# Group-norm statistics of three jobs on ScalarE, and weight batches, stores and sums at other steps of an attention pipeline

## The chip, the core and the metric

The kernel runs on one core of a Trainium2 chip. The metric is the device time of one execution in microseconds; lower is better. Engines are named as the profile names them: PE is TensorE (PEld its weight loads), DVE is VectorE, ACT is ScalarE, POOL is GpSimd, SP is SyncE, which issues most DMAs.

## The reference

Eight images of 512 channels and 32 x 32 positions, all float32, go through two layers. Each layer is a group norm over 8 groups, an attention with 8 heads of 64 channels over the 1024 positions, an output projection and a residual sum:

```
xg   = x.reshape(B, 8, -1)
xn   = (xg - xg.mean(-1)) * rsqrt(xg.var(-1) + 1e-5)      # then gamma, beta
q, k, v = Wq xn + bq, Wk xn + bk, Wv xn + bv              # 512 x 512 each
attn = softmax(q^T k / 8)                                  # per head, 1024 x 1024
x    = x + Wp (attn v) + bp
```

Layer 1 does the same with weights of its own. The output is x after both layers.

## The kernel before, in words

**Jobs.** A job is one image in one layer; there are 16, numbered n = 0 to 15, in the order image 0 layer 0, image 1 layer 0, image 0 layer 1, image 1 layer 1, then images 2 and 3 and so on. The program is a loop over n: the attention of job n, then the products that belong to the output projection O of job n and to V, K and Q of job n + 1. The order of instructions on PE, DVE and ACT is written out by hand; SP and POOL follow the program's order too.

**Projections.** The 512 x 512 weight products use Strassen's seven products at two levels, so each weight block is held as seven combined blocks per level. The combinations of the weights are made once for each layer by `factor` (L162 to L168, four DVE operations), stored to DRAM, and fetched again by later jobs (`w<-deep`, L189). From job 2 on V too has two levels (`DEEP_V = 2`); for job 1 it has one. On the side of the activations, `combine` (L423 to L429) makes the first level's sums of xn in the tile `t`, and `inner_sums` (L482 to L488) the second level's in the tile `deep`. Tiles of the name `round`, `raw` and `deep` share one buffer, in turns.

**Weight batches.** `put_round` (L1563) loads in jobs 0 to 3 one raw weight matrix for the round listed in `ROUNDS`, makes its factors by eight DVE operations, `first` and `second` (four of 128 x 512, four of 128 x 896), and stores seven tiles with DMAs on ACT's queue (`deep<-round`, L235). `put_first` (L1576) in jobs 0 and 1 loads one raw matrix (`raw<-wqkv_dram`), makes four factors (128 x 512) and stores them (`keep<-raw`).

**Attention.** `run` (L1258) goes through 64 steps: eight groups g (a pair of heads and half of the queries) of eight key blocks kc. Step i computes the scores of block i into a PSUM tile of two banks (two such tiles exist), ACT takes the exponential into a tile `e` (L1104), and PE multiplies the exponentials of step i - 2 with V (`po`, L1152). The 12 buffers of `e` are also those of the fetched weights and of partial products. The softmax sums are taken over the `e` tiles of a group: DVE adds them into `acc` (L1118, L1120), but the first `pairs(g)` pairs are first summed by POOL with an accumulating DMA (`e<-e`, L1129), and DVE adds each such sum at its due step, seven after (L1132). The last due add is followed by the reduction (L1190, `r`). Two groups share what follows: `gather` (three DMAs on SP, `r<-r`, L1213), about 7.6 us later by the program's own count `invert` (DVE, `lt` and on, L1217 to L1237, then DMAs `rd<-rt` and `rb<-rd`, L1230 and L1232), and `normalise` (DVE, L1247) at 16.2. `take` copies half of `po` on ACT (`px`, L1176) and adds on DVE (L1178).

**Beside attention.** Other work is put at given steps through tables: `put` fills `chores` (one function to a step; a taken step pushes the next one on), `move` fills `moves` (mostly DMAs). At step i `run` first does the attention's own work, then `chores[i]`, then `moves[i]`. Among it is the group norm of job n + 1 (class `Norm`):

- reads: `stat` (L279, bn_stats over 128 x 512 on DVE, then an aggregate L283), eight calls at steps 3 to 10, and `gather` (SP: `dm<-mv` L320, `gm<-dm` L324);
- `groups` (five small DVE operations, L331 to L335, a power on POOL, L336, and DMAs `dg<-ga` L338 and twice `mr<-dg` L341);
- `factors` (three small DVE operations, L349 to L351) and four times `apply` on ACT (L356, 128 x 1024);
- then the four `combine` sums.

The class also has a second way to read the statistics, which job 0 uses for a quarter of its channels: `sums` (L289, ACT, Identity with accumulation), `less_mean`, `squares` (L297, ACT, Square with accumulation and the negated mean as bias), `by_count`. Both write their element outputs into the tile `xn`, where `apply` overwrites them.

**After attention.** The last attention groups' sums, the output sums `os` (L593 to L598) and the partial products' additions follow on DVE, with a planner that keeps a clock of its own. Its entries are the same before and after.

Of the kernel before, what the change touches and what calls it, by code (L numbers as in the profile page):

```python
# [27 lines left out]
NC = C // P  # L28
# [25 lines left out]
DEEP_V = 2  # L54
ROUNDS = {0: (O, 0), 1: (V, 1), 2: (O, 1), 3: (V, 0)}
FIRST = {0: (K, 1), 1: (Q, 1)}
OUTER_V = (1, 6, 7, 2, 3, 5, 4)


# [22 lines left out]
def fast_path(  # L82
# [317 lines left out]
    def norm_steps(n):  # L400
        norm = Norm(n)

        def place():
            xn[0] = acts.tile([P, NC, S], F32, tag="xn", name=f"xn_{n}")

        def factors():
            norm.factors(slice(0, NC))
            place()

        reads = [lambda cc=cc, sh=sh: norm.stat(cc, sh) for cc in range(NC) for sh in range(2)]  # L410
        reads.append(norm.gather)
        steps = [norm.groups, factors] + [lambda cc=cc: norm.apply(cc) for cc in range(NC)]
        return reads, steps
# [664 lines left out]
    class Attention:  # L1078
# [43 lines left out]
        def pairs(self, g):  # L1122
            if g + 1 == len(self.groups):
                return 0
            return 3 if self.n < 2 and 0 < g < 5 else 2

        def add_pair(self, i):
            g, kc = self.steps[i]
# [126 lines left out]
            for at, step in zip(times, (gather, invert, spread, normalise)):  # L1255
                later(at, step)

        def run(self, chores, moves, taken=False):  # L1258


            steps = self.steps
            self.add(1)
            self.add(2)
            self.values(0)
            for at in (chores, moves):
                if 2 in at:
                    at[2]()
            for i in range(3, len(steps) + LEAD):
                if i < len(steps):
                    self.scores(i)  # L1270
                self.values(i - LEAD)
                g, kc = steps[i - LEAD]
                if kc % 2 == 1 and kc < 2 * self.pairs(g):
                    self.add_pair(i - LEAD)
                if i in self.due:
                    self.due.pop(i)()
                if kc == NT - 1:
                    if taken and g + 1 == len(self.groups):
                        self.reduce(g)
                    else:  # L1280
                        self.finish(g)
                    advance(0.85)
                for at in (chores, moves):
                    if i in at:
                        at[i]()
                advance(1.71)
# [141 lines left out]
    norm = Norm(0)  # L1428
# [116 lines left out]
    for n in range(-1, len(jobs)):  # L1545
        last = n + 1 == len(jobs)
        outs = None
        if n >= 0:
            chores, moves = {}, {}

            def put(i, fn):
                while i in chores:
# [9 lines left out]

            def put_round(which, layer):  # L1563
                load, first, second, stores = deep_round(which, layer)
                begin = {0: 6, 1: 12}.get(n, 9)
                move(begin, load)
                at = begin + 3
                for fn in first:
                    at = put(at + 1, fn)
                for fn in second:  # L1570
                    at = put(at + 1, fn)
                at = max(at + 3, 25)
                for i, fn in enumerate(stores):
                    at = move(at + 1 + i % 2, fn)

            def put_first(which, layer):  # L1576
                at = move(37 if n == 0 else 3, lambda: start()) + 3
                box = []

                def start():  # L1580
                    box.append(acts.tile([P, NW, 2, CH], F32, tag="deep", name=f"raw_{n}"))
                    load_blocks(box[0], layer, which)

                for part in range(4):
                    at = put(at + 1, lambda part=part: factor(box[0], part))
                move(at + 1, lambda: store_factors(box[0], layer, which))

            if last:
                w = last_weights(n)
                for part in range(4):  # L1590
                    put(12 + 2 * part, lambda part=part: factor(w, part))
                for i, fn in enumerate(last_sums(0)):
                    put(49 + 3 * i, fn)
            else:
                for i, (_, fn) in enumerate(extra):
                    put(2 + i, fn)
                if n == 1:
                    at = (8, 14, 15, 16, 18, 19, 21, 24, 27, 30)
                else:
                    for i, fn in zip((3, 3, 4, 5, 5, 6, 7, 7, 8), reads):  # L1600
                        put(i, fn)
                    at = (16, 22, 23, 24, 26, 27, 29, 31, 33, 35)
                    if n < DEEP_V + 2:
                        at = (17, 23, 24, 25, 27, 28, 30, 32, 34, 36)
                for i, fn in zip(at, steps):
                    put(i, fn)
                if n == 1:
                    put_first(*FIRST[n])
                if n in ROUNDS:
                    put_round(*ROUNDS[n])  # L1610
                if n == 0:
                    put_first(*FIRST[n])
                for i, fn in zip(at[len(steps) :], sums(n + 1)):
                    put(i, fn)
                put(48, lambda q=att.q: out_combine(q, None, 0))
                deep_first = deep_steps(n + 1)
                if n + 1 >= DEEP_V:
                    for i, fn in enumerate(deep_first):
                        put((42 if n in ROUNDS else 37) + 2 * i, fn)
                else:  # L1620
                    for at, fn in zip((50, 52, 54, 56), deep_first[4:]):
                        put(at, fn)
                move(58, lambda: extend_plan(n + 1))
                for _ in range(RING):
                    move(58, fetch)
            assert max([*chores, *moves], default=0) < NT * len(att.groups) + LEAD
            if n + 1 >= DEEP_V and not last:
                outs = OutputSums(n)
                ahead = deque()
                if jobs[n][1] == 1 and jobs[n][0] + 2 < B:  # L1630
                    ahead.extend(load_steps(jobs[n][0] + 2))
                both, plan_sums = deep_phases(n + 1, ahead, outs)

                att.run(chores, moves, True)
                extra = ahead
                plan_sums()
                banks(0, "one")
                if n + 2 < len(jobs):
                    reads, steps = norm_steps(n + 2)
                att.take(len(att.groups) - 1, both[0])  # L1640
                banks(1, "one")
                for thunk in both[1:]:
                    thunk()
                banks(0, "two")
                att = Attention(n + 1)
                att.scores(0)
                att.scores(1)
                banks(1, "two")
                att.scores(2, "po")
                continue  # L1650
            att.run(chores, moves)
            banks(0, "one")
            banks(1, "one")
            if last:
# [285 lines left out]
```

## Time and profile before

| what | value |
|---|---|
| median of 3 runs | 3186.69 us (3186.46 to 3188.62) |
| profiled execution, its own time | 3189.37 us |
| its span, first to last instruction | 3187.6 us |
| PE busy | 3155.9 us, 99% |
| DVE, ACT, POOL busy | 82%, 73%, 9% |
| mean granted PE clock | 0.997 |
| `w<-deep` fetches, `e<-e` sums, `deep<-round` stores | 399, 232, 28 DMAs |

Start and end of one execution of a job are easiest seen in the scores (L1099): step 3 of job 0 starts at 83.3 us, of job 1 at 293.0, of job 2 at 498.7, of job 3 at 699.1, of job 4 at 899.4, and from there every 195.6 us. A line of busy time by stretch gives the stretch, its length, then the busy time and the instructions in brackets for each engine, the granted PE clock, the DMA engines' busy share and GB/s. A line of waits gives the engine, the line that waited, what it waited for, the total in us, how often and the longest. A line of the timeline gives the start, the length, the engine, the line, the operation and, in square brackets, how long the engine had been idle and what released it.

### The profile page before, as it was taken

The numbers are of one execution on the slowest core, as the hardware profiler recorded it, in microseconds if no ns is written. First come the engines' busy times: TensorE is split into PE (matmuls) and PEld (weight loads), VectorE is DVE, ScalarE is ACT, GpSimd is POOL, SyncE is SP. The second block draws the span as 40 slices with busy tenths as digits, with TensorE's granted clock in tenths as the row PEclk, the third lists the DMA queues.
The fourth block names the chain that finished last, engine by engine and source line by source line (L and its number), as shares of the span: only waits on it lengthen the run. The fifth ranks groups of instructions, "written<-read, shape, count | busy, mean of one in ns | idle before, by whom it ended". The sixth has DMA issues, their size and how long they took to land.

```text
span 3187.6 us, 62162 instructions
## 1 busy us (share of the span) xinstructions
PE 3155.9 (99%) x24093; PEld 1873.2 (59%) x24093; DVE 2628.9 (82%) x3563; ACT 2334.8 (73%) x4234; POOL 290.8 (9%) x326
## 2 busy tenths in 40 slices
PE   9999999999999999999999999999999999999999
PEld 7366384573845738466393664837548375573844
DVE  8796798978979788797887969789697887978867
ACT  6657677686876868778687776867768677686874
POOL 0200101011000010100101010010000100001000
PEclk9999999999999999999999999999999999999999
DMA  7755765565645455355564545445556463444733
GB/s 276 165 141 156 161 204 137 150 195 134 203 106 142 122 101 183 73 147 164 130 199 81 157 101 143 125 94 170 136 140 179 88 193 75 132 127 95 221 75 82
DMA packets 187342, 454.51 MB, mean 143 GB/s; under 512 B 38056, under 2 KB 54304, under 8 KB 187040
## 3 DMA queue, kind: packets, MB, share of 16 engines
q0 software_dynamic: 50000, 153.64, 26.5%
q1 hardware_dynamic: 133008, 283.98, 26.2%
q10 hardware_dynamic: 4032, 12.85, 1.1%
q8 instruction: 192, 3.15, 0.4%
q14 instruction: 110, 0.90, 0.1%
HBM read 247.41 MB, written 48.17 MB: 93 GB/s over the span
## 4 chain that ended last, share of the span: by engine, by line
PE 76%; DVE 1%; issue 0%; ACT 0%; DVEq 0%
PE sc L1099 22%; PE po L1152 21%; PE zd L806 8%; PE vd L806 8%; PE yd L806 4%; PE ud L806 3%; PE vd L801 3%; PE zd L801 3%; PE yd L801 1%; PE ud L801 1%; DVE acc L1120 0%; PE z_last L1042 0%; DVE acc L1132 0%; DVE x L1064 0%; PE y_last L1042 0%
## 5 line engine op out<-in xcount | busy, mean ns | idle before, releaser
L1104 ACT ACTIVATE e<-sc 128x1024 f32<-128x1024 f32 x1024 | 1043.7, 1025 | 578.6 <-PE sc L1099 545.9
L1099 PE MATMUL sc<-q,k 64*64 64x512 f32 x8192 | 1059.8, 590 | 9.1 <-ACT e L1104 9.1
L1152 PE MATMUL po<-e,v 64*64 64x512 f32 x8192 | 1059.7, 590 | 5.1 <-ACT e L1104 5.1
L1152 PEld LDWEIGHTS po<-e,v 64*64 64x64 f32 x8192 | 312.7, 133 | 573.6 <-issue 543.4
L1099 PEld LDWEIGHTS sc<-q,k 64*64 64x64 f32 x8192 | 310.5, 133 | 575.2 <-issue 508.7
L1120 DVE TENSOR_TENSOR acc<-acc,e 128x1024 f32<-128x1024 f32 x304 | 370.1, 1217 | 38.2 <-ACT e L1104 28.5
L1129 POOL DMA_DIRECT2D e<-e x232 | 199.6, 860 | 1766.6 <-ACT e L1104 1460.3
L1132 DVE TENSOR_TENSOR acc<-acc,e 128x1024 f32<-128x1024 f32 x232 | 282.4, 1217 | 3.1 <-DMA e<-e 1.1
L1118 DVE TENSOR_TENSOR acc<-e,e 128x1024 f32<-128x1024 f32 x128 | 156.5, 1223 | 155.8 <-ACT e L1104 155.7
L806 PE MATMUL zd<-deep,w 128*128 128x256 f32 x860 | 240.2, 379 | 0.3 <-ACT ud L501 0.3
L806 PE MATMUL vd<-deep,w 128*128 128x256 f32 x804 | 223.5, 379 | 0.0
L806 PEld LDWEIGHTS zd<-deep,w 128*128 128x128 f32 x860 | 163.3, 190 | 22.9 <-ACT ud L501 0.7
L806 PEld LDWEIGHTS vd<-deep,w 128*128 128x128 f32 x804 | 152.8, 190 | 20.8
L1190 DVE TRANSPOSE_TENSOR_REDUCE r<-acc 128x32 f32<-128x1024 f32 x128 | 159.4, 1245 | 4.3
L901 POOL DMA_DIRECT2D x<-p x61 | 72.8, 1194 | 975.2 <-ACT p L823 492.0
L848 DVE TENSOR_TENSOR p<-p,s 128x512 f32<-128x512 f32 x185 | 127.5, 689 | 27.1 <-ACT p L823 21.2
L801 PE MATMUL vd<-w,deep 128*128 128x128 f32 x840 | 119.4, 276 | 0.0
L848 DVE TENSOR_TENSOR q<-q,s 128x512 f32<-128x512 f32 x64 | 44.2, 691 | 86.5 <-ACT q L825 45.1
L801 PE MATMUL zd<-w,deep 128*128 128x128 f32 x728 | 107.8, 277 | 2.3 <-ACT ud L501 2.3
L801 PEld LDWEIGHTS vd<-w,deep 128*128 128x128 f32 x840 | 106.6, 193 | 0.0
L806 PE MATMUL vd<-os,w 128*128 128x256 f32 x364 | 105.5, 379 | 0.0
L806 PE MATMUL zd<-os,w 128*128 128x256 f32 x356 | 99.0, 379 | 3.2 <-ACT yd L497 3.2
(296 smaller groups left out, 4827.1 us busy)
## 6 DMA issues: line engine op xcount, KB each, us to landing
w<-deep SPq DMA_DIRECT2D x399, 448.0 KB, 5.6
e<-e POOLq DMA_DIRECT2D x232, 512.0 KB, 4.7
x<-p POOLq DMA_DIRECT2D x61, 512.0 KB, 6.5
rb<-rd SPq DMA_DIRECT2D x96, 256.0 KB, 3.7
x<-x_dram SPq DMA_DIRECT2D x28, 512.0 KB, 3.6
out_dram<-x SPq DMA_DIRECT2D x28, 512.0 KB, 6.3
deep<-w SPq DMA_DIRECT2D x28, 448.0 KB, 2.7
deep<-round ACTq DMA_DIRECT2D x28, 448.0 KB, 5.5
```

The costliest lines, as they stand in the source:

```text
L801: nc.tensor.matmul(ps[:, tokens], moving[i][:, tokens], lhs[:, FACTOR[i], :], start=(start and ti == 0), stop=True, skip_group_check=True,)
L806: nc.tensor.matmul(ps, lhs[:, FACTOR[i], :], moving[i], start=start, stop=True, skip_group_check=True,)
L848: nc.vector.tensor_add(to_, to_, five.to_broadcast([P, 2, QT]))
L901: nc.gpsimd.dma_start(to_, p(part), accum_op=ALU.add)
L1099: nc.tensor.matmul(sc[h * HD : (h + 1) * HD, j, :], k[r, hp, k0 : k0 + HD], q[r, hp, sh * HALF : (sh + 1) * HALF], start=True, stop=True,)
L1104: nc.scalar.activation(e, sc, AF.Exp, scale=SCALE)
L1118: nc.vector.tensor_add(acc[g], self.es[i - 1], e)
L1120: nc.vector.tensor_add(acc[g], acc[g], e)
L1129: nc.gpsimd.dma_start(self.summed[i], self.summed.pop(i - 1), accum_op=ALU.add)
L1132: nc.vector.tensor_add(self.acc[g], self.acc[g], self.summed.pop(i))
L1152: nc.tensor.matmul(po[g][j * HD : (j + 1) * HD, h, :], v[r, kc, d0 : d0 + HD], e[r, j, :], start=(kc == 0), stop=(kc == NT - 1),)
L1190: nc.vector.tensor_reduce(self.r[:, 0, m, :], self.acc.pop(g).rearrange("p j (b e) -> p (j b) e", e=RP), AX.X, ALU.add, apply_transpose=True,)
```

## The change

- For n + 1 in `SCALAR` = (1, 3, 4), that is during the attention of jobs 0, 2 and 3, the statistics are read by ACT: four `sums` at steps 3 to 6, `less_mean` (DVE) at 7, four `squares` at 8 to 11, `by_count` (DVE) and `gather` at 12, through a third table, `aside`. The tile `xn` is taken at step 3 instead of with the factors.
- In these jobs `groups` stands at step 18 (17 before), `factors` at 26 (23), the applies at 27, 28, 30, 31 (24, 25, 27, 28), the sums of `combine` from 32 on. In job 1 `groups` stays at 8, factors go from 14 to 16, applies from 15-19 to 17-21.
- `pairs` gives three pairs for groups 1 to 4 in jobs 0 to 3, not only in jobs 0 and 1. The reductions of these groups in jobs 2 and 3 come two steps later.
- The round load: table step 6 to 3 in job 0, 12 to 13 in job 1 (where 12 was taken and it stood at 13), 9 to 5 in jobs 2 and 3. First of its factors at step 7 (12 before), 19 (17), 10 (13), 10 (13). First and last store at 17 and 26 (26 and 35 before) in job 0, 31 and 37 (30 and 39) in job 1, 20 and 29 (26 and 35) in jobs 2 and 3.
- The raw load: step 30 instead of 37 in job 0, with its factors at 35 to 38 and its store at 39 (45 before); 2 instead of 3 in job 1, with its store at 11 (12).
- `inner_sums` of the next job: 39, 41, ... 53 in job 1 and 37, 39, ... 51 in jobs 2 and 3, instead of 42 on in all three; 45, 46, 47, 49 in job 0 instead of 50, 52, 54, 56.

From job 4 on every engine's order is what it was.

```diff
--- before.py
+++ after.py
@@ -54,6 +54,7 @@
 DEEP_V = 2
 ROUNDS = {0: (O, 0), 1: (V, 1), 2: (O, 1), 3: (V, 0)}
 FIRST = {0: (K, 1), 1: (Q, 1)}
+SCALAR = (1, 3, 4)
 OUTER_V = (1, 6, 7, 2, 3, 5, 4)
 
 
@@ -407,6 +408,15 @@
             norm.factors(slice(0, NC))
             place()
 
+        if n in SCALAR:
+            reads = [lambda: (place(), norm.sums(0))]
+            reads += [lambda cc=cc: norm.sums(cc) for cc in range(1, NC)]
+            reads.append(norm.less_mean)
+            reads += [lambda cc=cc: norm.squares(cc) for cc in range(NC)]
+            reads.append(lambda: (norm.by_count(), norm.gather()))
+            return reads, [norm.groups, lambda: norm.factors(slice(0, NC))] + [
+                lambda cc=cc: norm.apply(cc) for cc in range(NC)
+            ]
         reads = [lambda cc=cc, sh=sh: norm.stat(cc, sh) for cc in range(NC) for sh in range(2)]
         reads.append(norm.gather)
         steps = [norm.groups, factors] + [lambda cc=cc: norm.apply(cc) for cc in range(NC)]
@@ -1122,7 +1132,7 @@
         def pairs(self, g):
             if g + 1 == len(self.groups):
                 return 0
-            return 3 if self.n < 2 and 0 < g < 5 else 2
+            return 3 if self.n in ROUNDS and 0 < g < 5 else 2
 
         def add_pair(self, i):
             g, kc = self.steps[i]
@@ -1255,14 +1265,14 @@
             for at, step in zip(times, (gather, invert, spread, normalise)):
                 later(at, step)
 
-        def run(self, chores, moves, taken=False):
+        def run(self, tables, taken=False):
 
 
             steps = self.steps
             self.add(1)
             self.add(2)
             self.values(0)
-            for at in (chores, moves):
+            for at in tables:
                 if 2 in at:
                     at[2]()
             for i in range(3, len(steps) + LEAD):
@@ -1280,7 +1290,7 @@
                     else:
                         self.finish(g)
                     advance(0.85)
-                for at in (chores, moves):
+                for at in tables:
                     if i in at:
                         at[i]()
                 advance(1.71)
@@ -1546,7 +1556,7 @@
         last = n + 1 == len(jobs)
         outs = None
         if n >= 0:
-            chores, moves = {}, {}
+            chores, moves, aside = {}, {}, {}
 
             def put(i, fn):
                 while i in chores:
@@ -1562,19 +1572,17 @@
 
             def put_round(which, layer):
                 load, first, second, stores = deep_round(which, layer)
-                begin = {0: 6, 1: 12}.get(n, 9)
+                begin, gap = {0: (3, 3), 1: (13, 3)}.get(n, (5, 4))
                 move(begin, load)
-                at = begin + 3
-                for fn in first:
+                at = begin + gap
+                for fn in first + second:
                     at = put(at + 1, fn)
-                for fn in second:
-                    at = put(at + 1, fn)
-                at = max(at + 3, 25)
+                at += 2
                 for i, fn in enumerate(stores):
-                    at = move(at + 1 + i % 2, fn)
+                    at = move(at + (1 if n == 1 else 1 + i % 2), fn)
 
             def put_first(which, layer):
-                at = move(37 if n == 0 else 3, lambda: start()) + 3
+                at = move(30 if n == 0 else 2, lambda: start()) + (4 if n == 0 else 3)
                 box = []
 
                 def start():
@@ -1595,13 +1603,15 @@
                 for i, (_, fn) in enumerate(extra):
                     put(2 + i, fn)
                 if n == 1:
-                    at = (8, 14, 15, 16, 18, 19, 21, 24, 27, 30)
+                    at = (8, 16, 17, 18, 20, 21, 22, 24, 26, 28)
+                elif n + 1 in SCALAR:
+                    for i, fn in enumerate(reads):
+                        aside[3 + i] = fn
+                    at = (18, 26, 27, 28, 30, 31, 32, 34, 36, 38)
                 else:
                     for i, fn in zip((3, 3, 4, 5, 5, 6, 7, 7, 8), reads):
                         put(i, fn)
                     at = (16, 22, 23, 24, 26, 27, 29, 31, 33, 35)
-                    if n < DEEP_V + 2:
-                        at = (17, 23, 24, 25, 27, 28, 30, 32, 34, 36)
                 for i, fn in zip(at, steps):
                     put(i, fn)
                 if n == 1:
@@ -1616,9 +1626,9 @@
                 deep_first = deep_steps(n + 1)
                 if n + 1 >= DEEP_V:
                     for i, fn in enumerate(deep_first):
-                        put((42 if n in ROUNDS else 37) + 2 * i, fn)
+                        put((39 if n == 1 else 37) + 2 * i, fn)
                 else:
-                    for at, fn in zip((50, 52, 54, 56), deep_first[4:]):
+                    for at, fn in zip((45, 46, 47, 49), deep_first[4:]):
                         put(at, fn)
                 move(58, lambda: extend_plan(n + 1))
                 for _ in range(RING):
@@ -1631,7 +1641,7 @@
                     ahead.extend(load_steps(jobs[n][0] + 2))
                 both, plan_sums = deep_phases(n + 1, ahead, outs)
 
-                att.run(chores, moves, True)
+                att.run((chores, moves, aside), True)
                 extra = ahead
                 plan_sums()
                 banks(0, "one")
@@ -1648,7 +1658,7 @@
                 banks(1, "two")
                 att.scores(2, "po")
                 continue
-            att.run(chores, moves)
+            att.run((chores, moves, aside))
             banks(0, "one")
             banks(1, "one")
             if last:
```

## The prediction

> **What bounds the kernel now.** First the page's busy line, then busy time cut at the starts of the jobs, then TensorE's waits in the stretches that stand out, then the order of time around one of them.
>
> ```profile
> PE 3155.9 (99%) x24093; PEld 1873.2 (59%) x24093; DVE 2628.9 (82%) x3563; ACT 2334.8 (73%) x4234; POOL 290.8 (9%) x326
> ```
>
> TensorE is named as the bound. What is left to win is where it isn't busy, or busy at half clock. So I cut the span from the third scores step of one job to that of the next (jobs 0 to 5):
>
> ```profile
> core 0: us, PE busy (x) PEld busy (x) DVE busy (x) ACT busy (x) POOL busy (x), PEclk, DMA share, GB/s
> 83.30:293.00 209.70, 199.13 (x1437) 115.57 (x1433) 166.50 (x238) 135.92 (x234) 24.98 (x23) 1.00 0.60 156
> 293.00:498.70 205.70, 199.28 (x1518) 119.20 (x1514) 170.70 (x264) 147.72 (x273) 20.79 (x23) 0.98 0.67 176
> 498.70:699.10 200.40, 197.52 (x1522) 116.91 (x1518) 168.33 (x221) 148.86 (x273) 19.45 (x20) 0.99 0.61 166
> 699.10:899.40 200.30, 197.55 (x1518) 115.30 (x1514) 168.91 (x221) 148.74 (x273) 18.24 (x19) 0.99 0.59 160
> 899.40:1095.00 195.60, 195.60 (x1519) 116.65 (x1515) 162.20 (x213) 148.17 (x273) 17.37 (x19) 1.00 0.49 124
> 1095.00:1290.60 195.60, 195.60 (x1522) 116.67 (x1518) 162.24 (x213) 148.60 (x273) 17.40 (x19) 1.00 0.50 124
> ```
>
> The reader sees that from job 4 on a job takes 195.6 us with TensorE never idle: nothing is to be had there. The first four take 14.1, 10.1, 4.8 and 4.7 us more. TensorE's idle time in them is 10.6, 6.4, 2.9 and 2.75 us. In jobs 1 to 3 the rest is half clock; in job 0 it is 3.5 us of busy time, of which about 0.5 us hangs on its stall (attention 107.0 against 103.0 us, 3.5 of it idle) and 3 us on its different V products. So the most that can be won is 4.0 + 7.1 in job 0, 10.1 in job 1 and 4.8 + 4.7 in jobs 2 and 3: 30.7 us. TensorE's waits in the first stretch and around the end of job 1's attention:
>
> ```profile
> PE sc L1099 <- ACT e L1104: 3.5, 2, 2.9
> PE zd L806 <- ACT yd L497: 3.2, 1, 3.2
> PE z L553 <- DVE v L579: 2.2, 1, 2.2
> PE po L1152 <- ACT e L1104: 1.1, 1, 1.1
> PE z L553 <- DMA w<-wqkv_dram: 0.7, 1, 0.7
> ```
> ```profile
> PE po L1152 <- ACT e L1104: 4.1, 1, 4.1
> PE zd L801 <- ACT ud L501: 2.3, 1, 2.3
> ```
>
> None of these is a slow ScalarE. The timeline at step 27 of job 2 (job 3 is its copy, job 0 nearly) shows who is behind:
>
> ```profile
> 537.39 0.59 DVE L1217 TENSOR_REDUCE lt<-r 32x64 f32<-32x256 f32 x1 [1.63 <-DMA r<-r]
> ...
> 540.56 0.16 DVE L351 TENSOR_TENSOR off<-vec_sb,off 128x4 f32<-128x4 f32 x1
> ...
> 540.76 1.24 ACT L356 ACTIVATE xn<-x,off,mul 128x1024 f32<-128x1024 f32 x1 [3.88 <-DVE off L351]
> ...
> 542.96 1.95 PE L1099 MATMUL sc<-q,k 64*64 64x512 f32 x8 [2.88 <-ACT e L1104]
> ```
>
> VectorE is late (bn_stats and the batches of factors came before), then stands for a tiny transfer; factors (step 23) end at 540.7; the first apply (step 24) holds ScalarE 3.88 us; the exponential behind it, and so scores 27, come late. At the end of job 1:
>
> ```profile
> 401.74 1.02 ACT L1104 ACTIVATE e<-sc 128x1024 f32<-128x1024 f32 x1 [5.35 <-DVE acc L1118]
> ```
>
> Exponential 63 waits for an e buffer that VectorE's add of step 57 frees: VectorE is 14.7 us behind TensorE's steps there, in job 0 11.7, in job 2 only 3.9.
>
> **What the Trainium skill says.** "TensorE: Matmul & The Clock Gate", What's actually happening: a free-running window of 3413 ns with too little work puts the array at half clock for one such window. The trace agrees: granted clock 0.50 in 403.2 to 406.4, 420.3 to 423.5, 543.1 to 546.4 and 744.5 to 747.7, each after a stall of 2.3 to 4.1 us, but none after the 2.9 and 3.2 us of job 0. So a removed stall can give 1.7 us more than its idle time. "ScalarE: Activation LUTs", What ACT_TABLE_LOAD costs: activations back to back overlap by about 93 ns; here an exponential of 1.02 us stands for 0.92. "DMA: Bandwidth & Descriptors", Issuing engines are not separate DMA queues: moving stores on ScalarE's queue still loads the same 16 engines as the small transfers; here the scale factors' way back (mr<-dg) took 2.2 us in calm stretches and some 7 us in job 0.
>
> **The change part by part.**
>
> *Statistics to ScalarE (jobs 0, 2, 3).* Removed from VectorE in steps 3 to 10: eight bn_stats of 0.69 us, spaced 0.60 behind others, and four aggregates, some 5.3 us a job; two tiny operations come in. Added to ScalarE in steps 3 to 11: four sums and four squares, seen once each in the start-up: 1.06 and 1.15 us plus a 0.19 us accumulator read that overlaps, so 1.05 and 1.15 us of queue. This lies beside TensorE only as far as slack goes. A step is 103.0/60 = 1.72 us, the exponential takes 0.92, so 0.80 is free. Sums put ScalarE back by 0.25 us a step, 1.0 after four; step 7 gives 0.8 back; squares add 0.35 each, and step 9 has a px copy of 0.46 besides: 1.4 late at step 10, in job 0 1.6, as square 0 waits some 0.2 us for less_mean behind a factor on VectorE. Exponential i starts 1.11 after its scores and ends at 2.13; scores i+2 need its bank at 3.43: about 1.2 us of slack. So TensorE loses 0.2 + 0.35 + 0.35, say 0.9 us (1.0 in job 0). Bounds: nothing, if the slack is 2 us; 2 us, if readings stand for their full lengths.
>
> *Eight steps for the power.* groups move from step 17 to 18, factors from 23 to 26, applies from 24 to 27. In job 2, groups end 4.2 us into step 18; power 0.6, dg and mr transfers some 3 to 4, landing 2.2 to 7: 10 to 16 us in. The first apply comes at 15.5 + 2.0 = 17.5. In job 0 the power took 4.6 us (0.56 elsewhere) and the landing 7: 18 us, within the 1.2 us of slack. SP's queue runs this ahead of the r gathers as before; those come two steps later too, as reductions move from 18 to 20. Factors are no longer behind lt by much, since VectorE is free: running up its queue gives a lateness of 4 us at step 26 instead of 6 to 7. The step 27 stalls go: 4.0, 4.8 and 4.7 us.
>
> *Three summed pairs in jobs 2 and 3 too.* Eight adds of 1.22 us leave VectorE, eight DMAs of 512 KB come on POOL. Jobs 0 and 1 have it already without a wait of note; on the path nothing.
>
> *Batches and their stores earlier.* The round load's place in SP's queue changes little: SP already ran ahead (in job 2 it issued at 495, before step 3). Factors of a round, 4 x 0.69 + 4 x 1.09 us, fill the stretch that bn_stats left. Stores (0.33 us of ScalarE's queue each, 448 KB, landing 5.5) go from steps 26-35 to 17-29, onto the mr and r transfers: I count 0.4 us of stall for job 0. In job 0 the raw weights load at 30 instead of 37, so its megabyte no longer meets the r gathers (VectorE waited 4.1 there) nor its stores the rb spread (4.35 at step 44). In job 1 the raw load and store lead by one step, round factors begin at 19 (VectorE waited 5.0 for that load at 17, now about 1.5), stores end at 37 instead of 39, and the deep sums start at 39, behind their landing.
>
> *What the transitions gain.* VectorE works nearly without a gap from its last wait until the stalls, so a stall shrinks by what it is less late. Job 0: waits of 4.1 + 0.7 + 4.35 us fall to about 4.5: some 4.5 of 7.1 us. Job 1: waits of 5.0 + 2.7 + 5.1 + 3.0 us; if transfers land as in job 2 (5.8 us after the reduction, 8 after the inversion), adding up the queue gives a lateness of 8 to 9 instead of 14.7 at step 57: past the 4.1 us stall, most of the 2.3 and both half clocks, 8 of 10.1. If they land as late as now, lateness is 14.0 and the gain 1. I take 8, since these transfers no longer meet as many SBUF-to-SBUF sums in flight.
>
> *Next sums at 37 to 51.* In jobs 2 and 3 the same eight operations; VectorE is 4 to 8 us late at step 57, under the 10 or so at which job 0 begins to stall: nothing.
>
> Sum: (4.0 - 1.0 - 0.4) + 4.5 + 8 + (4.8 - 0.9) + (4.7 - 0.9) = 22.8 us. The profiled execution took 3189.4 us (span 3187.6): 3166.6 on its scale. It stands 2.7 above the median, 3186.7, which gives 3163.9.
>
> **Rivals.**
> 1. *All stalls go.* ScalarE's slack takes the readings and VectorE is never late: 3186.7 - 30.7 = 3156. For it: jobs 4 to 15. Against: ScalarE's count above.
> 2. *The waits only change places.* VectorE arrives earlier at lt and rb and waits there, transitions keep their stalls: (4.0 + 4.8 + 4.7) - 3.2 + 2 = 12 us, 3174. For it: with landings as late as in job 1, the added-up queue ends equally late.
> 3. *The power is still late.* Stores and sums slow the mr transfer beyond 17.5 us, and step 27 stalls by half: 5 to 8 us won, 3180.
> 4. *Slower: the readings cost ScalarE more than slack.* Place: steps 3 to 11 of jobs 0, 2, 3. If a reading occupies p us, the loss is 3 x (8 x (p - 0.8) + 0.46 - 0.8 - 1.2). It eats the 25.5 us (22.8 and the readings' own 2.8) at p = 2.05; at p = 2.3 the kernel takes 3193. Against: 1.05 and 1.15 in the start-up, one reading each. The same sign follows if a store on ScalarE's queue has to wait for its batch.
> That the change does not do what it says is excluded: VectorE's queue loses the bn_stats of three jobs.
>
> **How the numbers follow.** A measurement of this kernel can tell about 0.2% (6.4 us) from no change. My forecast has 0.58 (3159 to 3169), rival 1 0.14 (3155 to 3159), rival 2 0.19 (3169 to 3177), rival 3 0.05, rival 4 0.04. Range 3156 to 3175. Faster by more than 0.2% (below 3180.3): 0.92; same 0.03 from rival 3; slower 0.05, rival 4 and its like.
>
> **What would show it.** Right: stretches cut at the same steps of about 202, 198, 197 and 197 us; no wait of ACT xn for DVE off at step 27; TensorE waits of 0.2 to 0.4 us at steps 10 to 13 of jobs 0, 2 and 3; clock 1.00 at 400 to 425. Wrong: VectorE still over 12 us late at the end of job 1; a TensorE wait over 1 us at steps 5 to 12; stretches of jobs 4 and later above 195.6.

## The result, and the profile after

The changed kernel is slower: 3196.7 us (median of 7 runs, 3194.8 to 3201.0) against 3186.9 us, a ratio of 1.0030 with an interval of 1.0018 to 1.0041. The forecast was 3163.9. The profiled execution has a span of 3196.1 us, 8.5 more than before. A ratio, here and below, is the recorded one and not the quotient of the two medians; the two differ by up to 0.07 per cent.

The page's busy line, and then busy time cut at the third scores step of each job, as in the prediction (columns: stretch, its length, busy time and number of instructions of each engine, granted clock, DMA share, GB/s):

```profile
PE 3159.4 (99%) x24093; PEld 1876.1 (59%) x24093; DVE 2602.5 (81%) x3525; ACT 2354.2 (74%) x4282; POOL 293.7 (9%) x334
```
```profile
core 0: us, PE busy (x) PEld busy (x) DVE busy (x) ACT busy (x) POOL busy (x), PEclk, DMA share, GB/s
83.00:292.20 209.20, 201.67 (x1435) 116.31 (x1431) 160.76 (x228) 143.43 (x250) 21.77 (x23) 0.99 0.61 156
292.20:494.00 201.80, 197.70 (x1518) 118.19 (x1514) 170.39 (x264) 147.38 (x273) 20.78 (x23) 0.99 0.68 180
494.00:700.40 206.40, 197.79 (x1522) 116.29 (x1518) 158.58 (x207) 155.25 (x289) 22.55 (x24) 1.00 0.65 171
700.40:907.20 206.80, 199.36 (x1522) 117.78 (x1518) 158.45 (x207) 155.46 (x289) 21.34 (x23) 0.99 0.62 165
907.20:1102.70 195.50, 195.50 (x1518) 116.63 (x1514) 161.98 (x213) 148.05 (x273) 17.39 (x19) 1.00 0.49 124
```

VectorE has 10 us less to do in jobs 2 and 3, as planned, and both take 6 us longer. Against before: job 0 -0.5, job 1 -3.9, job 2 +5.9, job 3 +6.5 us. From job 4 on nothing changed. TensorE's waits in the stretch of job 2, and a timeline of its steps 25 to 28 (start, length, engine, instruction, in brackets the idle time before it and what ended it):

```profile
PE sc L1109 <- ACT e L1114: 4.7, 3, 2.7
PE vd L811 <- DMA w<-deep: 1.4, 1, 1.4
PE zd L811 <- ACT ud L511: 1.1, 1, 1.1
PE vd L811 <- ACT ud L511: 1.1, 1, 1.1
```
```profile
535.21 0.58 ACT L1186 COPY px<-po 128x512 f32<-128x512 f32 x1
539.60 0.88 POOL L1139 DMA_DIRECT2D e<-e  x1 [6.59 <-issue]
539.66 0.33 ACTq L236 DMA_DIRECT2D deep<-round  x1
540.09 1.02 ACT L1114 ACTIVATE e<-sc 128x1024 f32<-128x1024 f32 x1 [4.30 <-DMA r<-r]
540.19 0.58 DVE L1227 TENSOR_REDUCE lt<-r 32x64 f32<-32x256 f32 x1 [5.81 <-DMA r<-r]
...
543.95 0.16 DVE L352 TENSOR_TENSOR off<-vec_sb,off 128x4 f32<-128x4 f32 x1
544.03 1.22 DVE L1142 TENSOR_TENSOR acc<-acc,e 128x1024 f32<-128x1024 f32 x1
544.15 1.24 ACT L357 ACTIVATE xn<-x,off,mul 128x1024 f32<-128x1024 f32 x1 [2.12 <-DVE off L352]
...
547.27 2.03 SPq L1242 DMA_DIRECT2D rb<-rd  x2
...
555.38 1.22 DVE L1257 TENSOR_TENSOR q<-q,rb 128x1024 f32<-128x1024 f32 x1 [8.85 <-DMA rb<-rd]
```

Three things are to be seen. A store (539.66) stood at the head of ScalarE's queue, and the exponential of step 26 behind it lost 4.30 us. What it waited for is in the semaphores that the trace keeps: the transfers of SP and ScalarE share eight completion semaphores, and this store waits on the one that it will use itself, which the second r gather of SP still held (issued 532.81, landed 539.64). VectorE stood 5.81 us for those gathers, so the factors and the first apply were late again (2.12). And the rb transfer took 8 us from its first issue, so VectorE stood another 8.85 us. It was 10.3 us late at step 55 (4.1 before), and the transition to job 3, 92.6 us without a wait, took 97.0.

The gathers are three transfers of 8 KB. They took 5.7 to 6.8 us each from issue to landing, 2.2 to 3.9 before. What lay beside them shows in the windows of 529 to 538 us, of the kernel after and then of the kernel before (the last but one column is the share of the 16 DMA engines):

```profile
529.00:532.00 3.00, 3.00 (x35) 1.06 (x28) 0.10 (x1) 2.05 (x2) 0.60 (x1) 1.00 1.03 231
532.00:535.00 3.00, 3.00 (x36) 1.06 (x28) 2.35 (x2) 1.73 (x2) 0.86 (x1) 1.00 1.13 246
535.00:538.00 3.00, 3.00 (x36) 0.91 (x24) 0.00 (x0) 0.79 (x2) 0.00 (x0) 1.00 1.03 271
```
```profile
529.00:532.00 3.00, 3.00 (x32) 1.07 (x28) 2.97 (x4) 2.05 (x2) 0.50 (x1) 1.00 0.70 134
532.00:535.00 3.00, 3.00 (x32) 1.07 (x28) 3.00 (x4) 1.82 (x2) 0.86 (x1) 1.00 0.85 157
535.00:538.00 3.00, 3.00 (x32) 1.07 (x28) 1.35 (x2) 1.25 (x2) 0.00 (x0) 1.00 0.44 74
```

After the change the DMA engines are full for 9 us, with stores of 448 KB and pair sums of 512 KB under way, while the gathers are in flight. The Trainium skill, "DMA: Bandwidth & Descriptors", Issuing engines are not separate DMA queues, says that DMAs issued by different engines run on the same 16 DMA engines and interleave. The prediction cited it for just this, and the windows agree; what was wrong was the size I gave it.

### The profile page after: what moved, and what is told of

It reads as the page before. It is cut to its first block, busy times and chain, and to the rows that moved or that the text cites. A ratio compares the mean times of both kernels' runs of the same rounds, so it can differ in the third digit from the quotient of the medians.

```text
span 3196.1 us, 62182 instructions
## 1 busy us (share of the span) xinstructions
PE 3159.4 (99%) x24093; PEld 1876.1 (59%) x24093; DVE 2602.5 (81%) x3525; ACT 2354.2 (74%) x4282; POOL 293.7 (9%) x334
## 4 chain that ended last, share of the span: by engine, by line
PE 86%; DVE 6%; DMA 3%; issue 2%; ACT 2%; SPq 1%; POOL 0%; ACTq 0%; DVEq 0%; POOLq 0%
PE sc L1109 23%; PE po L1162 23%; PE zd L816 11%; PE vd L816 11%; PE yd L816 5%; PE ud L816 4%; PE vd L811 3%; PE zd L811 3%; DVE acc L1130 1%; PE ud L811 1%; PE yd L811 1%; DVE acc L1142 1%; ACT e L1114 1%; DMA rb<-rd 1%; DMA r<-r 1%
## 5 line engine op out<-in xcount | busy, mean ns | idle before, releaser
L1109 PE MATMUL sc<-q,k 64*64 64x512 f32 x8192 | 1059.3, 590 | 13.6 <-ACT e L1114 12.8
L1130 DVE TENSOR_TENSOR acc<-acc,e 128x1024 f32<-128x1024 f32 x288 | 350.6, 1217 | 39.6 <-ACT e L1114 30.0
L1142 DVE TENSOR_TENSOR acc<-acc,e 128x1024 f32<-128x1024 f32 x240 | 291.7, 1216 | 1.8
L1257 DVE TENSOR_TENSOR q<-q,rb 128x1024 f32<-128x1024 f32 x64 | 77.1, 1205 | 39.4 <-DMA rb<-rd 38.6
```

Of the source, the lines that this page charges most:

```text
L1109: nc.tensor.matmul(sc[h * HD : (h + 1) * HD, j, :], k[r, hp, k0 : k0 + HD], q[r, hp, sh * HALF : (sh + 1) * HALF], start=True, stop=True,)
L1130: nc.vector.tensor_add(acc[g], acc[g], e)
L1142: nc.vector.tensor_add(self.acc[g], self.acc[g], self.summed.pop(i))
L1257: nc.vector.tensor_mul(place, place, box[0])
```

## The experiments

In what follows "stretch" is a job's time between third scores steps, "attention" the part of it from step 3 to 63, "transition" the rest, and lateness is how far VectorE's add of step 55 starts behind that step's scores. One caution, since each version has one trace: job 0 of the changed kernel is the same code in three more of these kernels and took 209.2, 209.8, 210.5 and 211.5 us, and job 3 of two other versions, again the same code, took 200.1 and 203.3. A difference of up to 3 us in a single stretch proves nothing by itself.

### Parts of the change undone

**Late stores.** Jobs 0, 2 and 3.

```diff
-                at += 2
+                at = at + 2 if n == 1 else max(at + 2, 25)
```

> The changed kernel with one thing undone: in jobs 0, 2 and 3 the seven stores of the batches begin at step 26 again instead of 17 to 20. Theory A (the early stores are the loss: their 448 KB each lie on the DMA engines when the small r gathers run, and one of them stands at the head of ScalarE's queue until a gather lands): the stalls at steps 28 to 31 of jobs 0, 2 and 3 go but for the readings' own 1.4 us at steps 11 to 14, VectorE is under 8 us late at step 57 of jobs 2 and 3, stretches of about 203, 202, 198 and 198 us, total 3174 to 3180. Theory B (the third summed pair in jobs 2 and 3 is the loss): only the wait on ScalarE's queue goes, some 2 us a job, VectorE stays 10 us late in jobs 2 and 3, total about 3190. Theory C (the readings on ScalarE are the loss): unchanged within 3 us, 3194 to 3199.

Measured 3198.2 us, ratio 1.0037 (1.0024 to 1.0050). Stretches 214.9, 203.0, 204.1 and 202.1. In jobs 2 and 3 that is 2.2 and 4.7 us less than in the changed kernel, the first within the spread, and the exponential of step 26 no longer waits. Job 0 loses 6: its raw load at step 30 goes into the buffer that the stores still read, SP stands from 130.5 to 148.8 us with the next r gathers behind it, and VectorE is 16.5 us late at step 39. So theory A holds for jobs 2 and 3 in part, and job 0's raw load needs its early stores.

**Two pairs in jobs 2 and 3.**

```diff
-            return 3 if self.n in ROUNDS and 0 < g < 5 else 2
+            return 3 if self.n < 2 and 0 < g < 5 else 2
```

> The changed kernel with one thing undone: jobs 2 and 3 have two summed pairs a group again, as before the change, and so their r gathers two steps earlier. Theory A (early stores): the stores still meet the gathers, the stall at steps 26 to 30 of jobs 2 and 3 stays over 3 us, total 3188 to 3196. Theory B (third pair): stretches of jobs 2 and 3 fall from 206 to about 198 us, that of job 0 stays at 209, total about 3180. Theory C (readings): unchanged within 3 us.

Measured 3188.0 us, ratio 1.0005 (0.9997 to 1.0013): with this alone the change is neutral. Jobs 2 and 3, columns as in the first windows:

```profile
495.80:696.80 201.00, 197.44 (x1518) 116.08 (x1514) 163.22 (x211) 155.13 (x289) 18.62 (x20) 1.00 0.61 165
696.80:897.40 200.60, 197.23 (x1518) 116.14 (x1514) 163.07 (x211) 155.57 (x289) 17.41 (x19) 1.00 0.58 159
```

The third pair so cost 5.3 and 6.2 us there, in company of the rest of the change; no other part undone gave as much back. With two pairs the gathers go out two steps earlier (the first 33.3 us after step 3 of job 2 instead of 37.5), and lateness is 8.0 and 6.2 instead of 10.3 and 11.0.

**Both undone.**

> The changed kernel with both undone: stores of jobs 0, 2 and 3 begin at step 26, two summed pairs in jobs 2 and 3. Theory A: within 2 us of the run with late stores alone, 3174 to 3180. Theory B: within 2 us of the run with two pairs alone in jobs 2 and 3. If both count, it is the fastest of the three, with VectorE under 5 us late at step 57 of jobs 2 and 3 and stretches there of 197 to 198 us, total about 3172.

Measured 3192.6 us, ratio 1.0018 (1.0011 to 1.0024); job 0 is as bad as with late stores alone (216.2). Jobs 2 and 3 take 197.9 and 200.1 us, 15 us less than in the changed kernel. The pair has 11.5 of them. What late stores add beside two pairs is 3.1 and 0.5 us, so the stores' share in the time is not settled. That both slow the gathers is plainer: from the first issue of an r gather to lt, which waited for it each time, jobs 2 and 3 take 8.7 and 8.9 us in the changed kernel, 6.7 and 6.7 with late stores, 5.9 and 7.5 with two pairs, 5.0 and 6.5 with both, and 4.4 and 5.4 before the change.

**Stores on GpSimd's queue.**

```diff
-            nc.scalar.dma_start(keep, box[0][:, FACTOR[o]])
+            nc.gpsimd.dma_start(keep, box[0][:, FACTOR[o]])
```

> The changed kernel with the stores of the batches issued by GpSimd instead of ScalarE, at the same steps: the transfers load the engines as before, but nothing of ScalarE waits behind them. If the cost is the store standing at the head of ScalarE's queue: no wait of an exponential of over 1 us at steps 25 to 27, attention of jobs 0, 2 and 3 falls by 2 to 4 us each, total 3185 to 3190. If the cost is the load on the DMA engines, which makes gathers, lt and rb late: VectorE stays 10 us late at step 57 of jobs 2 and 3, the pair sums behind the stores on GpSimd's queue come later too, total 3193 to 3200 or more.

Measured 3214.4 us, ratio 1.0087 (1.0073 to 1.0101), worse than both expectations. No exponential waits for a gather any more, but four wait 13.8 us for pair sums. In job 0 lt waits 12.5 us for r, the first apply 12.8 us for its factors, and VectorE waits 23 us over jobs 0 to 3 for pair sums that now stand behind stores (it had no such wait of note). In job 0 SP's queue shows where the gathers lost more: the raw load waits 10.6 us for the stores, the power's result (dg) leaves behind it at 127.0 and lands at 135.0, and mr and the r gathers, next in the queue, leave at 135.1 and 136.8. So this run puts new waits in the place of the old one, and does not tell how much of the loss was ScalarE's queue.

**Statistics by VectorE.** The readings alone go back to `bn_stats`, at their old steps.

> The changed kernel with one thing undone: the statistics of jobs 1, 3 and 4 are read by VectorE (bn_stats) again, at the steps they had; all other steps stay. Theory C (readings cost ScalarE): the slow steps 11 to 14 of jobs 0, 2 and 3 vanish (1.87, 1.28 and 1.28 us). VectorE has some 5 us more to do by step 12, but it waited 2.9 us or more at steps 15 and 23 of jobs 2 and 3, so nothing is later from step 24 on: stretches of about 207.3, 201.8, 205.0 and 205.5 us, total 3192. If instead VectorE's free time was needed (theory D: the readings pay for themselves), steps 26 to 30 get worse by 2 us or more a job and the total is 3196 to 3204.

Measured 3195.0 us, ratio 1.0024 (1.0016 to 1.0031), span 3192.9, 3.2 less. The slow steps 11 to 14 are gone, 4.4 us in all; at steps 28 to 32 jobs 0, 2 and 3 lose 6.9, 7.1 and 6.0 us instead of 3.9, 4.9 and 4.5, which is 6.6 more. The attentions are so some 2 us longer in all, and the transitions of jobs 2 and 3 6.3 us shorter, with VectorE 6.0 and 8.9 us late instead of 10.3 and 11.0. Theories C and D each have a part that fits. But more moved than the readings: back in VectorE's table they push the batches on, so that the first store leaves 35.6 us after step 3 instead of 28.0 in job 0 and 31.8 in jobs 2 and 3, and the power takes 2.4 us instead of 1.4. The interval overlaps that of the changed kernel as well, so what the readings alone are worth is not shown.

**Job 1's next sums at 42.**

```diff
-                        put((39 if n == 1 else 37) + 2 * i, fn)
+                        put((42 if n == 1 else 37) + 2 * i, fn)
```

> The changed kernel with the next deep sums of job 1 from step 42 again instead of 39. In the changed kernel VectorE stands 3.82 us at the first of these sums (for the stores of the round), then 0.5 us for lt at step 40. If the early sums only moved a wait: VectorE waits at step 40 for lt instead, its lateness at step 55 stays 12 us or falls by no more than 1, stretch of job 1 201 to 203 us, total 3195 to 3198. If they lost time: lateness at step 55 falls to 9, the stretch to 199, total 3193. If they gained time: stretch 204 or more.

Measured 3202.4 us, ratio 1.0044 (1.0031 to 1.0058). Job 1 takes 205.4 us, 3.6 more and nearly the 205.7 of before; in the changed kernel and ten versions with the same code for it job 1 took 201.6 to 203.0. The earlier sums are the whole gain of job 1. Its lateness at step 55 hardly moves (12.7 and 12.2); but the last sum then stands at step 56, ahead of the adds that free the e buffers.

### Parts of the change alone, in the kernel before

**Third pair alone.**

> The kernel before with one part of the change alone: three summed pairs a group in jobs 2 and 3 as well. If the third pair costs by itself (eight more transfers of 512 KB, the r gathers two steps later and behind them): VectorE over 8 us late at step 55 of jobs 2 and 3, stretches there 204 to 206 us instead of 200.4, total 3195 to 3199. If it costs only together with early stores and readings: 199 to 201.5 us, total within 2 us of before; if the eight adds saved count, 197 to 199 and 3183.

Measured 3193.2 us, ratio 1.0014 (1.0007 to 1.0020). Columns as in the first windows, jobs 2 and 3:

```profile
501.10:704.10 203.00, 198.12 (x1522) 118.44 (x1518) 164.08 (x217) 147.88 (x273) 23.55 (x24) 0.99 0.66 174
704.10:904.90 200.80, 197.59 (x1522) 118.40 (x1518) 163.87 (x217) 147.69 (x273) 22.34 (x23) 0.99 0.63 170
```

The pair does two things at once. The step 27 stall vanishes (attention 103.1 instead of 107.8 us): the factors now end ahead of lt (38.2 and 39.3 us after step 3 of job 2; before, lt stood at 38.7 and the factors ended at 42.0). And lateness grows to 12.0 and 10.2 us; the transitions, 92.6 before, take 99.8 and 97.7. VectorE's waits for transfers in job 2:

```profile
DVE q L1247 <- DMA rb<-rd: 7.8, 2, 4.6
DVE lt L1217 <- DMA r<-r: 3.6, 1, 3.6
DVE acc L1132 <- DMA e<-e: 2.6, 3, 1.3
```

In the kernel before only one of 1.6 us, for r, stood there. Loss and gain nearly cancel in these two stretches (2.6 and 0.4 us longer than before), so the pair alone costs less than it does beside early stores and readings.

**Power's eight steps alone.** Only the list of steps is changed, as in the change (groups 18, factors 26, applies 27, 28, 30, 31).

> The kernel before with another part alone: groups at step 18, factors at 26, applies from 27 in jobs 0, 2 and 3; statistics on VectorE, batches and stores, pairs as before. As predicted for the change (the power's landing no longer holds VectorE, the first apply finds its factors): the step 27 stall goes, attention 103 to 104 us, stretches of jobs 0, 2 and 3 of 206, 196.5 and 196.5 us, total 3175. If the factors now stand behind lt, take, adds and the reduction, as in the changed kernel: a stall of 1 to 3 us at steps 28 to 31 takes its place, stretches of 207 to 208, 198 to 199 and 198 to 200 us, total 3180 to 3184.

Measured 3195.0 us, ratio 1.0025 (1.0018 to 1.0031): slower by itself. The attentions of jobs 0, 2 and 3 take 110.0, 110.2 and 111.2 us. ScalarE's wait around step 27 of job 2, and how it comes about:

```profile
ACT xn L356 <- DVE off L351: 6.3, 1, 6.3
```
```profile
529.16 1.07 DVE L164 TENSOR_TENSOR round<-round 128x896 f32<-128x896 f32 x1
...
529.38 5.56 POOL L336 TENSOR_TENSOR ga<-gv,neg_half 8x1 f32<-8x1 f32 x1 [11.34 <-DVE gv L335]
...
533.30 1.21 DVE L1120 TENSOR_TENSOR acc<-acc,e 128x1024 f32<-128x1024 f32 x1
...
534.97 0.30 SPq L338 DMA_DIRECT2D dg<-ga  x1
535.32 0.51 SPq L1213 DMA_DIRECT2D r<-r  x1
...
539.58 0.59 DVE L1217 TENSOR_REDUCE lt<-r 32x64 f32<-32x256 f32 x1 [5.07 <-DMA r<-r]
```

GpSimd's power on 8 numbers takes 5.56 us, until VectorE's run of two-operand operations ends. Now that groups stand at step 18, its result's way out (dg) stands on SP's queue ahead of the third r gather. So the gather leaves at 535.3, lt waits 5.07 us, and the factors at step 26, behind lt and 5 us of other work, end at 547.2. The power was given more steps and took VectorE's inversion with it.

### Repairs

**Late stores and two pairs in jobs 2 and 3 only.**

> The changed kernel with stores from step 26 and two summed pairs in jobs 2 and 3 only; job 0 keeps its early stores, since its raw weights load at step 30 had to wait for late ones (GpSimd and SP stood, VectorE 17 us late at step 40 in the run with late stores). Stretches of 209.3, 201.9, 198 and 200 us as in the runs that had each: total 3181 to 3183, 5 us faster than before the change. If jobs depend on one another (a late end of job 0 or 1 moves the collisions of the next), up to 3187.

Measured 3185.9 us, ratio 0.9994 (0.9985 to 1.0002). Stretches 211.5, 201.6, 197.9 and 203.3; job 3, the same code as in the run with both undone (200.1), lost 6.1 us at steps 30 to 32, where it had lost 2.3 there.

**Factors right behind the inversion,** step 24 instead of 26 in jobs 0, 2 and 3 of that kernel.

```diff
-                    at = (18, 26, 27, 28, 30, 31, 32, 34, 36, 38)
+                    at = (18, 24, 27, 28, 30, 31, 32, 34, 36, 38)
```

> As the run before with late stores and two pairs in jobs 2 and 3, and the scale factors at step 24 instead of 26 in jobs 0, 2 and 3: on VectorE they then stand right behind the inversion (lt) and ahead of two adds, a take and a reduction, 4 to 5 us of queue. If the rest of the stall at steps 28 to 31 is that the first apply waits for factors behind this queue: it goes in jobs 2 and 3 (the factors end at about 743 instead of 747.8 us on job 3's clock, and the exponential of step 27 ends at 745), attention there 104.5 us (the readings' 1.3 left), and shrinks by 1.8 us in job 0; total about 3176. If the mr values are not there yet, or the applies themselves cost the steps: unchanged, 3182.

Measured 3182.4 us, ratio 0.9986 (0.9977 to 0.9995). Around step 27 of job 3:

```profile
738.76 0.16 DVE L352 TENSOR_TENSOR off<-vec_sb,off 128x4 f32<-128x4 f32 x1
...
739.00 1.23 ACT L357 ACTIVATE xn<-x,off,mul 128x1024 f32<-128x1024 f32 x1
```

The apply has no wait before it. Jobs 2 and 3 take 197.2 and 197.6 us, and the only slow steps of their attention are the readings'. This shows what held the apply in jobs 2 and 3: the place of its factors in VectorE's queue, not the power. By the ratios the two kernels are not told apart (the intervals overlap).

**Readings spaced,** in the version with factors at step 24.

```diff
-                    for i, fn in enumerate(reads):
-                        aside[3 + i] = fn
+                    for i, fn in zip((3, 4, 5, 6, 7, 8, 10, 11, 13, 14), reads):
+                        aside[i] = fn
```

> As the run with late stores, two pairs (jobs 2 and 3) and factors at step 24, and the readings spaced: sums at steps 3 to 6, the mean at 7, squares at 8, 10, 11 and 13, the gather at 14 (instead of squares at 8 to 11, the gather at 12). By the count of ScalarE's queue (0.80 us free in a step; a sum takes 1.05, a square 1.15, a copy 0.46) it is never over 1.2 us late: the slow steps 11 to 14 vanish, 1.3 us in each of jobs 2 and 3 and 1.9 in job 0; stretches of jobs 2 and 3 196 us, total 3178. If the gather two steps later makes the factors late: a wait of the first apply at step 27 of 1 to 3 us and 3181 to 3185.

Measured 3193.3 us, ratio 1.0015 (1.0007 to 1.0024). The slow steps 11 to 14 are nearly gone (0.15 us left in jobs 2 and 3), as counted, but the transitions of jobs 2 and 3 took 97.4 and 98.9 us with VectorE 11 to 12 us late, and job 0 stalled for 8.9 us at steps 25 to 27.

**Job 0 as before, readings spaced,** and then **the same with readings close together**: load of the batch at step 6, stores from 26, raw load 37, sums 50 to 56 in job 0. Its readings stay on ScalarE, its factors for the applies at step 24.

> As the run with spaced readings, and job 0's batches, stores, raw weights load and next sums at the steps they had before the change (batches from 6, stores from 26, raw load 37, sums at 50 to 56). If their earlier place costs (stores onto the r gathers, the raw load onto the rb spread): job 0 takes 205.7 us (209.7 less the step 27 stall), with no stall at 26 to 31; total 3173 to 3175. If their earlier place gains the transition's 2 to 4 us as predicted: its attention falls to 103.5, but the transition is 102.7 again and the stretch 206 to 208, total 3175 to 3178. If VectorE gets later than before: over 210.

> The run with factors at step 24 (late stores and two pairs in jobs 2 and 3, readings close together), and in it only job 0's batches, stores, raw load and next sums put back to where they were before the change. Theory: their earlier place costs job 0 (its early stores meet the r gathers), and the spaced readings, not job 0, cost jobs 2 and 3 their transition (the statistics' gather two steps later moves the power beside another two-operand operation of VectorE, and the rb transfer into the stores). Then: job 0 206.3 + 1.6 for the close readings = 208 instead of 212, jobs 2 and 3 197.2 and 197.6 as in the run with factors at step 24; span 3175 to 3177. Rival: job 0's end moves the collisions of jobs 2 and 3, which stay at 199 and 202: 3182 to 3185.

Measured 3187.4 us, ratio 0.9998 (0.9990 to 1.0006), and 3185.3 us, ratio 0.9986 (0.9978 to 0.9994). Job 0 takes 206.3 and 208.9 us, with no stall at 26 to 31; with close readings jobs 2 and 3 are at 197.6 and 197.7 again, against 199.3 and 202.1. So the spaced readings, not job 0, moved the collisions. In the traces the power starts beside an add (1.43 instead of 0.56 us), and the rb of job 3 lands 10 us after its issue, among the stores, instead of 4.7 as in the run with factors at step 24; which of the two counts more was not separated.

**Readings from step 2,** the gather left at 12: steps 2 to 5, 6, 7, 8, 10, 11, 12.

> As the run just before, with the readings one step earlier and spaced without moving the statistics' gather: sums at steps 2 to 5, mean 6, squares 7, 8, 10, 11, gather 12. If only ScalarE's queue counts: no slow steps at 11 to 14, 1.3 to 1.9 us less in jobs 0, 2 and 3, span 3171 to 3173. If the exact place of the transfers decides more than the queue, stretches of jobs 2 and 3 of 199 to 202 us again: 3178 to 3184.

Measured 3180.7 us, ratio 0.9981 (0.9974 to 0.9988), the lowest of all and faster than both kernels, though its interval overlaps those of the two versions at 0.9986. Its profiled execution, jobs 0 to 3:

```profile
83.30:288.20 204.90, 200.83 (x1438) 116.61 (x1434) 161.72 (x228) 143.40 (x250) 21.77 (x23) 0.99 0.61 159
288.20:490.50 202.30, 198.24 (x1522) 118.17 (x1518) 170.36 (x264) 147.34 (x273) 20.78 (x23) 0.99 0.68 180
490.50:686.70 196.20, 196.02 (x1522) 116.31 (x1518) 163.45 (x211) 155.51 (x289) 18.62 (x20) 1.00 0.63 169
686.70:884.30 197.60, 196.76 (x1522) 116.21 (x1518) 163.05 (x211) 155.28 (x289) 17.41 (x19) 1.00 0.59 162
```

Jobs 2 and 3 are within 0.6 and 2.0 us of a job without a wait: spaced readings cost them nothing when the statistics' gather keeps its step. By its ratio the version wins some 6 us over before. The profiled execution, with a span of 3172.8 us, was the fastest of its 21 (3174.6 to 3187.3 us), so its stretches flatter it.

## Why the prediction was wrong, by its own steps

Two terms failed. The third pair, put at nothing on the path, cost 11.5 us in jobs 2 and 3. And the step 27 stalls, booked as gone, came back as 13.3 us at steps 28 to 31; the two overlap, since some 4 us of these went with the pair. In both, the prediction took the r gathers and rb to land as before, though the moves put them later and among more traffic; and it left the factors behind lt and 5 us of adds in VectorE's queue.

- **What can be won** (30.7 us in jobs 0 to 3, and no more): no run speaks against it. The last version, which keeps the readings on ScalarE, the later power and job 1's part, has about half of it (15.2 us) in its profiled execution, its fastest.
- **Readings:** predicted 1.0, 0.9 and 0.9 us at steps 10 to 13; measured 1.9, 1.3 and 1.3 at steps 11 to 14. The mechanism was right, and so was the slack of 1.2 us (in job 2 scores 12 came 0.64 us late behind an exponential that was 1.9 late). What was missed is that the first square waits for the mean, 0.52 us in job 2 while VectorE is at an add, and 1.12 in job 0; the prediction had this for job 0 alone, as 0.2.
- **The step 27 stalls go:** this failed. They had cost 3.9, 4.8 and 4.8 us; 3.9, 4.9 and 4.5 us appear at steps 28 to 31. "Factors are no longer behind lt by much" was the wrong sentence. It counted VectorE's own work and took lt as on time. The waits had changed place, as rival 2 said, though rival 2 still counted 12 us won.
- **Stores "onto the mr and r transfers", 0.4 us for job 0 and nothing for jobs 2 and 3:** the right collision, mis-sized. Late stores gave 2.2 and 4.7 us back in jobs 2 and 3 with three pairs, 3.1 and 0.5 with two. It missed that a gather delayed by 3 us delays lt, the factors, rb and VectorE in turn. That a store can wait on ScalarE's queue stood only in an aside to rival 4, and it waited for a gather, not for its batch.
- **"Three summed pairs: on the path nothing":** the largest error. It weighed eight adds against eight transfers by jobs 0 and 1, "without a wait of note". But jobs 0 and 1 end 12 to 15 us late. The pair moves the gathers two steps on, among more transfers, and cost 11.5 us in jobs 2 and 3 of the changed kernel; alone in the kernel before it made the whole slower too (1.0014).
- **Job 0's transition, 4.5 us:** 2.4, from 102.7 to 100.3 us; the attention took that back.
- **Job 1, 8 us with lateness of 8 to 9 at step 57:** 3.9, with 11.1 there. The round load still kept VectorE 4.2 us (1.5 expected), and the sums at 39, put "behind their landing" (of the stores), stood 3.8 us. TensorE's first stall (4.1) fell to 0.4, but a weight fetch then came 2.7 us late, and the half clock stayed (0.59 in 402 to 406).
- **The sums at 37 in jobs 2 and 3, nothing:** not tried alone. With late stores, two pairs and factors at 24 the transitions there are 92.8 and 93.3 us, so little can hang on them.

In sum -22.8 us was predicted for the four jobs and +8.0 measured: readings 1.6 more, stalls at 28 to 31 13 more, jobs 0 and 1 6.2 less won at the transitions, those of jobs 2 and 3 9.7 longer. Of the signs named beforehand as "wrong" one is on the border: VectorE is 12.2 us late at step 55 of job 1, but 11.1 at step 57, where the 14.7 of before was read. The kernel became slower, but not as rival 4 mainly had it: the readings cost 4.4 us at steps 11 to 14, where it needed more than 25.5.

## What to carry to other kernels

When work is moved, ask of each small transfer that a busy engine stands for what will lie on the DMA engines and ahead of it on its issuing queue at its new time. A total of busy time freed says little while an in-order engine still stands behind that transfer. A wait removed from one step has to be followed to the next thing in the same queue: here moving three tiny operations in front of 5 us of adds took the stall of jobs 2 and 3 away, where taking 5 us of work a job from VectorE had not.

## What the runs showed of the hardware

GpSimd's power on 8 x 1 took 0.56 us beside a VectorE add with one operand in PSUM (job 1 of both kernels). When an operation of two SBUF operands was already running it took 1.42 us with one of them (job 2 of both kernels), 2.42 with two in a row (third pair alone), 4.62 with four (job 0 of the kernel before) and 5.56 with five (power's eight steps alone), each time ending 0.43 or 0.44 us after the last. When the power started 0.15 us before such an add (two pairs, job 2), it took 0.57. The Trainium skill, "SBUF — State Buffer", Who interferes with whom, states that a VectorE instruction with two SBUF inputs contends with a GpSimd instruction that reads SBUF, and that issue order decides who blocks. The traces agree, and add that a run of such instructions back to back keeps GpSimd out to its end. The 4.6 us of job 0 in the kernel before, which the prediction took as it stood, was this.
